# Attention scores dealt into ten visits a batch instead of twelve, over seven PSUM banks

## The chip, the cores and the metric

The kernel runs on one core of one Trainium2 chip. The metric is the time of one execution in microseconds (us) of device time; of several runs the median is given. Beside it stands a profile of one execution, which names every instruction with its engine, its line and its times. TensorE is called PE there, its weight loads PEld, VectorE DVE, ScalarE ACT, GpSimd POOL and SyncE SP.

## The reference

Every batch `b` of 32 holds 256 channels of 32 x 32 = 1024 tokens. They are normalized in groups of 8 channels, projected to queries, keys and values, and go through causal attention with 8 heads of 32 channels, in which a token sees only those before it; the result is added to the input.

```python
xf = _gn(x).reshape(B, C, S)                       # B 32, C 256, S 1024, all float32
q = einsum('oc,bcs->bos', q_w, xf) + q_b           # 8 heads x 32 channels
k, v = split(einsum('oc,bcs->bos', kv_w, xf) + kv_b)
mask = tril(ones((S, S)), -1)
scores = where(mask == 0, -10000, q k^T / sqrt(32))
attn = where(mask == 0, 0, softmax(scores))
out = x + attn v
```

## The kernel before

**Tiles of the array.** All matmuls are float32. A score product (`score`, L325) takes 32 rows (the channels of one head) and 64 columns (half of a block of 128 keys): the array is split into 8 tiles of 32 x 64, one for each of four heads and each half of a key block, and they work side by side. Projections (`project_qk` L264, `project_v` L280) and products with the values (`values`, L441) use tiles of 128 x 32, four side by side. Scores are laid out transposed: keys on partitions, queries along the row, so that one product of a tile is a run of query columns for 64 keys. Each product stands in the profile as two weight loads and two matmul records.

**Visits.** A batch has two groups `g` of four heads. The lower triangle of key blocks and query columns is dealt to six visits a group (`VISITS`, L612), twelve a batch (`N`). A visit has a long run of 512 query columns for each head and a short one of 256 columns (two of the six), or of 192 where a pair of diagonal blocks shares the room (`pair`, L309). For each tile this comes to 704 columns in visits 0, 1, 3 and 4 and to 768 in visits 2 and 5.

**PSUM.** `ps_s` has three buffers of two banks each. A visit takes all three: long runs of heads 0 and 1, long runs of heads 2 and 3, and the short runs of all four. Heads share a bank in the short runs, and tiles of different heads must not write one bank at the same time, so `scores` (L375) issues the short products of heads 2 and 3 first, lets them raise the semaphore `bank_free`, and has PE wait once for it before the short products of heads 0 and 1. The two banks left are `ps_o`, which gathers the products with the values (`acc`), and `ps_m` (`misc`), in which the projections are made; a few early ones use `ps_o` (`spare`, L161).

**The order of the work** is written out by hand (`manual_schedule`): each engine runs its instructions in the order in which the program issues them. In step `i` of the main loop (L785) come: the scores of visit `i`, with three exponentials on ACT (two of the long runs, L426, then the short one, L422) and the masking of diagonal blocks on POOL (L366); what is due `at` step `i`, above all one projection, which ACT copies out of PSUM (L276, L293); the products of visit `i - 1` with the values (`PRODUCTS`, L624); the additions of its exponentials to a running sum on DVE (`ADDS`, L639; L469); and what is due `after` it. `PROJECT` (L681) gives the steps of the twelve projections of a batch, five of them before the batch's own first step. Other lists place the loads, the normalization, the folding of the sums by DMA from POOL and SP and the last division on DVE. In the last batch the sums are made on PE instead (`sums`, L508).

Of the kernel before, what the change touches and what calls it, by code (L numbers as in the profile page):

```python
# [26 lines left out]
HALFBANK = HALF // 2  # L27
ROW = 64
# [4 lines left out]
def tile_norm_attention_residual(  # L33
# [69 lines left out]
    def unshifted():  # L103
        live = {}
        bank_free = tc.alloc_semaphore("bank_free")
# [15 lines left out]
        qkpool = tc.alloc_tile_pool(name="qkpool", bufs=3)  # L121
# [6 lines left out]
        pools = [xpool, work, qkpool, epool, small, dram, ps_s, ps_o, ps_m]  # L128

        def misc(name):  # L130
            return ps_m.tile([P, HALF], F32, tag="misc", name=name)


        def load_weights(junk):
# [5 lines left out]
            for n, w in enumerate((q_w, kv_w[0:C], kv_w[C : 2 * C])):  # L140
                live["wn", n] = epool.tile([P, 4, HALFBANK], F32, tag="eh", bufs=3, name=f"wn_{n}")[:, :NG, :C]
                nc.sync.dma_start(out=live["wn", n], in_=w.rearrange("(o p) c -> p o c", p=P))
# [17 lines left out]

        def spare(name):  # L161

            live["turn"] = live.get("turn", -1) + 1
            if live["turn"] in (1, 3, 5):
                return ps_o.tile([P, HALF], F32, tag="acc", name=name)
            return misc(name)
# [52 lines left out]
        def norm_mean(b):  # L219
            mv = live["mv", b]  # L220
            pm = misc(f"pm_{b}")
# [12 lines left out]
        def norm_variance(b):  # L234
            pv = misc(f"pv_{b}")
# [28 lines left out]
        def project_qk(b, g, n, hf):  # L264
# [5 lines left out]
            pp = spare(f"pp_{b}_{g}_{n}_{hf}")  # L270
# [9 lines left out]
        def project_v(b, n):  # L280
# [4 lines left out]
            pp = spare(f"ppv_{b}_{n}").rearrange("p (s c) -> p s c", c=C)  # L285
# [9 lines left out]
        def projections(b):  # L295

            qk = [[lambda g=g, hf=hf, n=n: project_qk(b, g, n, hf) for n in range(2)] for g in range(NG) for hf in range(NH)]
            v = [lambda n=n: project_v(b, n) for n in range(NB // 2)]
            return qk[0] + v[:1] + qk[1][:1] + v[1:2] + qk[1][1:] + qk[2] + v[:1:-1] + qk[3]

        def full(kb, first, width, at):

            return at, width, [[(c, kb, first, width, slice(at, at + width))] for c in (0, KEYS)]

        def pair(j, at):  # L309


            even, odd = 2 * j, 2 * j + 1
            c0, c1, c2, c3 = (at + n * KEYS for n in range(4))
            return at, 3 * KEYS, [
                [
                    (0, even, even * P, P, slice(c1, c3)),
                    (0, odd, odd * P, KEYS, slice(c0, c1)),
                ],
                [
                    (KEYS, odd, odd * P, P, slice(c0, c2)),  # L320
                    (KEYS, even, even * P + KEYS, KEYS, slice(c2, c3)),
                ],
            ]

        def score(b, g, bank, j, op):  # L325

            c, kb, first, width, cols = op
            rows = slice(HD * j, HD * (j + 1))
            return nc.tensor.matmul(  # L329
                bank[c : c + KEYS, cols], lhsT=live["k", b, g][rows, kb * P + c : kb * P + c + KEYS],  # L330
# [3 lines left out]
        def scores_of(b, g, bank_of, heads, entries, between=lambda: None, order=slice(None)):  # L334

            done = {}
            for _, _, halves in entries:
                for k, n in enumerate(list(range(max(map(len, halves))))[order]):
                    if k:
                        between()  # L340
                    for j in heads:
                        for c, ops in enumerate(halves):
                            if n < len(ops):
                                done.setdefault((j, c), []).append(score(b, g, bank_of(j), j, ops[n]))
            return done

        def part_of(b, g, bank, entry, of):

            at, _, halves = entry
            for j in (0, 1):  # L350
                for ((c, kb, first, _, cols),) in halves:
                    score(b, g, bank[:, j, :], j, (
                        c, kb, first + of.start, of.stop - of.start, slice(cols.start + of.start, cols.start + of.stop)
                    ))

        def mask(b, g, raw, j):


            hf, place = j // 2, (2 * j % 4) * P
            if ("e", b, g, "D", hf) not in live:  # L360
                live["e", b, g, "D", hf] = epool.tile(
                    [P, 4, HALF], F32, tag=("e0", "e")[hf], bufs=4, name=f"diagonal_{b}_{g}_{hf}"
                )
            square = live["e", b, g, "D", hf]
            for s in range(2):
                nc.gpsimd.affine_select(  # L366
                    out=square[:, :, place + s * P : place + (s + 1) * P],
# [612 lines left out]
```

## Time and profile before

| | |
|---|---|
| time, median of 3 runs (1792.47 to 1795.82) | 1792.5 us |
| span of the profiled execution, first to last instruction | 1791.2 us |
| PE busy | 1782.1 us |
| DVE busy | 1669.4 us |
| ACT busy | 1441.4 us |
| POOL busy | 897.9 us |

The span of the profiled execution is 1.3 us below the median. Busy time counts an engine as busy from the start of an instruction to its recorded end, and a matmul's end is modelled, so that a PE that is always busy need not be at its peak: what PE does is read from the starts of its phases in the timeline. The timeline merges neighbouring instructions of one line; its columns are the start, the length, the engine, the line and the operation, the tiles, and the count. Where one row joins several shapes, it carries the name of one of them.

### The profile page before, as it was taken

How to read it: one execution, taken by the hardware profiler on the slowest of the kernel's cores; microseconds unless marked ns; L12 is line 12 of the kernel's file. 1: busy time of each engine (PE TensorE's matmuls, PEld its weight loads, DVE VectorE, ACT ScalarE, POOL GpSimd, SP SyncE). 2: the span in 40 equal slices, each digit the busy share in tenths (PEclk: the TensorE clock that was granted, in tenths of full speed). 3: DMA queues.
4: the chain of work that ended last, by engine and by line, in shares of the span. 5: the costliest groups of instructions: out<-in, count | busy, mean ns of one | idle time of the engine just before them, and what ended most of it. 6: DMA issues, size and time to landing. Idle time of an engine off the chain costs nothing.

```text
span 1791.2 us, 81784 instructions
## 1 busy us (share of the span) xinstructions
PE 1782.1 (99%) x37036; PEld 936.1 (52%) x37036; DVE 1669.4 (93%) x1796; ACT 1441.4 (80%) x1928; POOL 897.9 (50%) x935
## 2 busy tenths in 40 slices
PE   9999999999999999999999999999999999999998
PEld 5555555555555555555555555555555555555554
DVE  4689999999999999999999999999999999999998
ACT  6888878888778788788887888877888878888785
POOL 2355554554555555545555555454455554554542
PEclk9999999999999999999999999999999999999999
DMA  2567766767677676676776676767766766777663
GB/s 72 105 117 142 137 133 135 148 138 147 128 142 138 137 141 138 132 144 142 142 138 134 137 142 138 150 129 140 139 145 131 141 136 135 149 138 141 133 109 98
DMA packets 92771, 240.21 MB, mean 134 GB/s; under 512 B 26272, under 2 KB 27792, under 8 KB 76544
## 3 DMA queue, kind: packets, MB, share of 16 engines
q0 software_dynamic: 17360, 100.58, 40.1%
q1 hardware_dynamic: 74912, 134.28, 25.9%
q8 instruction: 290, 4.75, 1.1%
q14 instruction: 65, 0.53, 0.1%
q10 hardware_dynamic: 144, 0.07, 0.0%
HBM read 69.90 MB, written 34.95 MB: 59 GB/s over the span
## 4 chain that ended last, share of the span: by engine, by line
PE 99%; DVE 0%; ACT 0%; issue 0%; POOL 0%; POOLq 0%
PE sT L329 31%; PE acc L451 28%; PE pp L173 27%; PE ppv L173 13%; PE pd L503 1%; PE busy L159 0%; PE wt L152 0%; ACT e L426 0%; DVE rb_last L576 0%; DVE rb_last L563 0%; DVE turned L560 0%; DVE acc L573 0%; DVE inv_last L562 0%; POOL ident masks.py:199 0%; PE pv L173 0%
## 5 line engine op out<-in xcount | busy, mean ns | idle before, releaser
L426 ACT ACTIVATE e<-sT 128x1024 f32<-128x1024 f32 x768 | 744.3, 1022 | 301.5 <-PE sT L329 298.8
L366 POOL TENSOR_SCALAR_AFFINE_SELECT diagonal<-eh 128x512 f32<-128x512 f32 x512 | 563.3, 1122 | 625.4 <-ACT eh L422 624.7
L469 DVE TENSOR_TENSOR e<-e,e 128x1024 f32<-128x1024 f32 x314 | 578.0, 1841 | 23.0 <-ACT v L293 3.5
L329 PE MATMUL sT<-q,k 32*64 32x64 f32 (+1 forms) x18928 | 577.9, 367 | 0.1
L329 PEld LDWEIGHTS sT<-q,k 32*64 32x64 f32 x18928 | 397.0, 131 | 203.8 <-PE sT L329 67.4
L173 PE MATMUL pp<-xn,wT 128*32 128x512 f32 x4096 | 492.3, 598 | 0.0
L451 PE MATMUL acc<-e,v 128*32 128x512 f32 (+3 forms) x4608 | 401.0, 450 | 0.0
L422 ACT ACTIVATE eh<-sT 128x768 f32<-128x768 f32 (+1 forms) x384 | 341.6, 890 | 0.0
L451 PEld LDWEIGHTS acc<-e,v 128*32 128x32 f32 x4608 | 149.2, 110 | 261.5 <-issue 239.0
L173 PE MATMUL ppv<-wT,xn 128*32 128x256 f32 x4096 | 247.5, 382 | 0.0
L469 DVE TENSOR_TENSOR diagonal<-diagonal,e 128x1536 f32<-128x1536 f32 x126 | 194.5, 1544 | 16.1 <-PE acc L451 6.5
L173 PEld LDWEIGHTS pp<-xn,wT 128*32 128x32 f32 x4096 | 107.0, 109 | 195.8 <-issue 163.7
L469 DVE TENSOR_TENSOR e<-e,eh 128x1024 f32<-128x1024 f32 x126 | 177.6, 1410 | 6.5
L451 PEld LDWEIGHTS acc<-diagonal,v 128*32 128x32 f32 x4096 | 120.9, 110 | 88.1 <-issue 68.2
L173 PEld LDWEIGHTS ppv<-wT,xn 128*32 128x32 f32 x4096 | 120.2, 109 | 80.0 <-issue 7.0
L469 DVE TENSOR_TENSOR e<-e,diagonal 128x2048 f32<-128x2048 f32 x63 | 144.0, 2285 | 18.9 <-POOL diagonal L366 18.7
L451 PE MATMUL acc<-diagonal,v 128*32 128x128 f32 x4096 | 158.9, 273 | 0.0
L205 POOL DMA_INDIRECT eight<-each,group_of x31 | 42.9, 1383 | 193.4 <-DMA each<-st 193.4
L262 ACT ACTIVATE xn<-x,shift,rstd 128x256 f32<-128x256 f32 x248 | 137.2, 614 | 0.8 <-POOL shift L247 0.8
L576 DVE SCALAR_TENSOR_TENSOR rb<-num,v_bias_col,x 128x256 f32<-128x256 f32 x248 | 121.5, 530 | 4.4
L482 POOL DMA_DIRECT2D e<-e x124 | 103.6, 835 | 42.6 <-issue 42.6
L482 POOL DMA_DIRECT2D diagonal<-diagonal x124 | 105.1, 847 | 0.7
(87 smaller groups left out, 1092.2 us busy)
## 6 DMA issues: line engine op xcount, KB each, us to landing
x<-in_x_dram SPq DMA_DIRECT2D x124, 256.0 KB, 3.8
diagonal<-diagonal POOLq DMA_DIRECT2D x62, 512.0 KB, 6.1
e<-e POOLq DMA_DIRECT2D x62, 512.0 KB, 5.7
rb<-inverses SPq DMA_DIRECT2D x124, 256.0 KB, 4.0
out_dram<-rb SPq DMA_DIRECT2D x124, 256.0 KB, 4.2
diagonal<-diagonal POOLq DMA_DIRECT2D x62, 256.0 KB, 4.6
folded<-diagonal SPq DMA_DIRECT2D x62, 256.0 KB, 5.1
e<-e POOLq DMA_DIRECT2D x62, 256.0 KB, 4.6
```

The costliest lines, as they stand in the source:

```text
L173: nc.tensor.matmul(out[part], lhsT=lhsT[:, part], rhs=rhs, start=start, stop=stop, skip_group_check=True)
L205: nc.gpsimd.indirect_dma_start(eight, None, live["each", b].rearrange("(m c) s -> m (c s)", c=CPG), bass.IndirectOffsetOnAxis(ap=group_of[ ...
L262: nc.scalar.activation(to, of, AF.Identity, bias=live["shift", b][:, g : g + 1], scale=rstd)
L329: return nc.tensor.matmul(bank[c : c + KEYS, cols], lhsT=live["k", b, g][rows, kb * P + c : kb * P + c + KEYS], rhs=live["q", b, g][rows, ...
L366: nc.gpsimd.affine_select(out=square[:, :, place + s * P : place + (s + 1) * P], in_=raw[:, :, (1 - s) * KEYS : (3 - s) * KEYS], pattern=[ ...
L422: exp = nc.scalar.activation(eh.rearrange("p (n bank) q -> p bank n q", n=2)[:, :, :, :narrow], short[:, :, :, :narrow], AF.Exp)
L426: nc.scalar.activation(e[:, 2 * a : 2 * a + 2, :wide], pairs[a][:, :, :wide], AF.Exp)
L451: nc.tensor.matmul(acc[HD * j : HD * (j + 1), of], lhsT=live["v", b][:, kb, h * HD : (h + 1) * HD], rhs=e[:, j, :], start=first, stop=last ...
L469: nc.vector.tensor_add(to, to, tile_of(b, g, at))
L482: nc.gpsimd.dma_start(out=total[:rows], in_=total[rows : 2 * rows], accum_op=ALU.add)
L503: nc.tensor.matmul(pd[HD * j : HD * (j + 1), of], lhsT=pick, rhs=e[:, j, :], start=start, stop=stop, skip_group_check=True,)
L576: nc.vector.scalar_tensor_tensor(blocks(rb, s), blocks(num, s, (start + s) % 2 == 1), v_bias_col[:, g : g + 1], blocks(xt[:, g, cols], s), ...
```

## The change

Each group of heads is visited five times instead of six, with 896, 832, 896, 896 and 896 columns for each tile. The score banks are four in `ps_s` (two buffers of two banks, long runs) and three in the new `ps_t` (`tri`): the short runs of the four heads, up to 384 columns each, lie one behind the other over three banks, so that heads 1 and 2 have pieces in two banks. The order of a visit's products is written as a string: `2e1` is the piece `e` of head 2 in bank 1 of `tri`, `3La` and `3Lb` are the first and the second half of head 3's long run, and `W` is a wait of PE for semaphore `bank_free[0]`, then `bank_free[1]`. The first pair of heads named (`sooner`) takes the first buffer of `ps_s`.

The bank `misc` is gone. A projection is made in a new buffer of `ps_s` (`room`), which is the one that held the visit's first two long runs, or in the bank of `acc` (`lone`). The products of the visit before with the values are split: one part ahead of the projection and one behind it. Visit 0 has no products of its own; visit 1 has those of both. At steps 1 and 6 of a batch there are two projections, `lone` and then `room`.

Key block rows 0 and 1 are masked where they stand; three pairs of blocks (2 and 3, 4 and 5, 6 and 7) share their room. DVE makes twelve additions a group instead of eleven, over the same number of columns, and in the last batch all but the last two visits' sums are made by additions, with fewer summing products on PE. Some pools have one buffer less (`qkpool`, `num`, `e`), the steps of all that is placed by hand are dealt anew for `N` = 10, and two waits before the values (`EVEN`) and the splitting of long runs in two visits (`SPLIT`) are gone.

```diff
-        bank_free = tc.alloc_semaphore("bank_free")
+        bank_free = [tc.alloc_semaphore(f"bank_free_{k}") for k in range(2)]
...
-        ps_s = tc.alloc_tile_pool(name="ps_s", bufs=3, space=PSUM)
+        ps_s = tc.alloc_tile_pool(name="ps_s", bufs=2, space=PSUM)
+        ps_t = tc.alloc_tile_pool(name="ps_t", bufs=1, space=PSUM)
         ps_o = tc.alloc_tile_pool(name="ps_o", bufs=1, space=PSUM)
-        ps_m = tc.alloc_tile_pool(name="ps_m", bufs=1, space=PSUM)
...
+        def lone(name):
+            return ps_o.tile([P, HALF], F32, tag="acc", name=name)
+
+        def room(name):
+            at = live.pop("room", None)
+            if at is None:
+                at = ps_s.tile([P, 2, HALF], F32, tag="sT", name=name)
+                live["room"] = at
+                return at[:, 0, :]
+            return at[:, 1, :]
...
+            early = [lone] if b == 0 else []
+            return [
+                qk(0, 0, 0, *early), qk(1, 0, 0), v(0, *early), v(1), qk(0, 0, 1), qk(1, 0, 1, lone),
+                qk(0, 1, 0), qk(1, 1, 0), v(2), v(3), qk(0, 1, 1), qk(1, 1, 1, lone),
             ]
...
+        def row(kb, blocks, more=()):
+            return [
+                ("o", 0, 0, kb + 1, (kb + 1) * P, KEYS), ("o", KEYS, 0, kb + 1, (kb + 1) * P, P),
+                ("e", 0, KEYS, kb, kb * P, blocks * P),
+                ("e", KEYS, P, kb, kb * P + KEYS, blocks * P - KEYS),
+            ] + list(more)
...
+            banks = [ps_s.tile([P, 2, HALF], F32, tag="sT", name=f"sT_{name}_{a}") for a in range(2)]
+            tri = ps_t.tile([P, 3 * HALF], F32, tag="tri", name=f"tri_{name}")
...
+                if isinstance(op, int):
+                    live["free", op] = live.get(("free", op), 0) + list(ends.values()).count(op)
+                    wait = nc.tensor.wait_ge(bank_free[op], live["free", op])
...
+            for a in range(2):
+                step = heads[a][1] - heads[a][0]
+                nc.scalar.activation(e[:, heads[a][0] : heads[a][1] + 1 : step, :], banks[a], AF.Exp)
+            exp = nc.scalar.activation(
+                eh[:, :, :wide], tri.rearrange("p (j q) -> p j q", q=SHORT)[:, :, :wide], AF.Exp
             )
...
+        WHOLE = "1s0 2s1 3s2 0L 2L 1L 3L W 0s0 1s1 W 2s2"
         VISITS = [
...
+            (0, 0, both("s", 1, P, 3 * P), (0, 2), WHOLE),
+            (0, HALF, row(2, 2), (2, 3), "2e2 1e1 3La 0e0 0o0 3Lb 2L 1L 0L W 3e2 3o2 2e1 W 1o0 2o1 1e0"),
+            (
+                1, HALF, row(4, 1, both("x", 5, 6 * P, P + KEYS, P + KEYS)), (2, 3),
+                "1e1 2x2 0x0 3Lb 0o0 1x1 2Lb 0e0 3La 1Lb 2La W 0Lb 3o2 1La 3x2 W 2o1 0La 2e1 1o0 3e2 1e0 2x1",
+            ),
+            (
+                2, HALF, row(6, 2, both("x", 5, 7 * P + KEYS, KEYS, 2 * P + KEYS)), (0, 1),
+                "3x2 1o0 2o1 0Lb 1e0 2e1 3e2 1Lb 3o2 0La 2Lb 1La 3Lb W 0o0 2La 0e0 3La 1e1 0x0 W 2e2 2x2 1x1",
+            ),
+            (3, HALF, both("s", 4, 5 * P, 3 * P), (0, 2), WHOLE),
         ]
...
-        PROJECT = (-5, -4, -3, -2, -1, 0, 1, 2, 3, 4, 5, 6)
-        PREPARE = (-12, -11, -10, -10, -9, -8, -7, -6, -5, -3)
-        SUMS = (3, 7, 10, 13)
+        PROJECT = (-4, -3, -2, -1, 0, 1, 1, 2, 3, 4, 5, 6)
+        PREPARE = (-11, -10, -9, -9, -8, -7, -6, -5, -2, -1)
+        SUMS = (4, 6, 8, 11)
+        STACK = (6, 9, 11, 14)
...
                 if i < B * N:
                     scores(*divmod(i, N))
+                b, v = divmod(i - 1, N)
...
+                if i:
+                    values(b, v, 0)
                 for f in at.pop(i, ()):
                     f()
...
                 if i:
-                    for _ in range(EVEN.count((i - 1) % N) if i < B * N - N else 0):
-                        nc.tensor.wait_ge(bank_free, live["free"])
-                    values(b, v)
-                    if b < B - 1 or v not in SUMMED or v == 1:
+                    values(b, v, 1)
+                    if b < B - 1 or v < N - 2:
                         add_keys(b, v)
```

The products with the values of the visits: visit 1 has 512 and 384 columns ahead of the projection and three of 128 behind it, visits 2 and 3 have 512 and 512 (visit 3 behind it in four pieces), visit 4 has 512 and 384, and three of 128.

More of the change, by code (lines that the diff above doesn't have):

```diff
@@ L27 @@
 HALFBANK = HALF // 2
+SHORT = 3 * P
 ROW = 64
@@ L540, in with_scores @@
         def with_scores(ahead=0):
-            nc.sync.wait_ge(bank_free, live["free"] + 4 * ahead)
+            v = live["visit"]
+            more = [n for i in range(v + 1, v + 1 + ahead) for n in PROGRAMS[i % len(VISITS)][1].values()]
+            nc.sync.wait_ge(bank_free[0], live["free", 0] + more.count(0))
         def spread_inverses(b, h):
```

376 lines of the change are left out of this document (181 added, 195 removed).

## The prediction

> **What bounds the kernel now.** I read the page's first section, then the timeline of PE over a few visits in the middle, then the engine windows of one batch.
>
> ```profile
> span 1791.2 us, 81784 instructions
> PE 1782.1 (99%) x37036; PEld 936.1 (52%) x37036; DVE 1669.4 (93%) x1796; ACT 1441.4 (80%) x1928; POOL 897.9 (50%) x935
> ```
>
> ```profile
> 899.23 1.49 PE L329 MATMUL sT<-q,k 32*64 32x64 f32 x64
> 900.65 1.92 PE L173 MATMUL pp<-xn,wT 128*32 128x512 f32 x16
> 902.39 1.05 PE L451 MATMUL acc<-e,v 128*32 128x384 f32 x16
> ...
> 903.80 1.47 PE L329 MATMUL sT<-q,k 32*64 32x128 f32 x48
> 905.21 1.92 PE L173 MATMUL pp<-xn,wT 128*32 128x512 f32 x16
> 906.95 1.05 PE L451 MATMUL acc<-e,v 128*32 128x384 f32 x16
> ...
> 908.36 1.55 PE L329 MATMUL sT<-q,k 32*64 32x256 f32 x32
> 909.84 1.92 PE L173 MATMUL pp<-xn,wT 128*32 128x512 f32 x16
> 911.58 0.61 PE L451 MATMUL acc<-e,v 128*32 128x256 f32 x8
> ...
> 912.56 1.46 PE L329 MATMUL sT<-q,k 32*64 32x64 f32 x56
> 913.95 1.93 PE L173 MATMUL ppv<-wT,xn 128*32 128x256 f32 x32
> 915.70 1.47 PE L451 MATMUL acc<-e,v 128*32 128x512 f32 x16
> ...
> 917.53 1.46 PE L329 MATMUL sT<-q,k 32*64 32x64 f32 x56
> ...
> 954.21 1.49 PE L329 MATMUL sT<-q,k 32*64 32x64 f32 x64
> ```
>
> ```profile
> 899.20:954.20 55.00, 55.00 (x1156) 28.86 (x1152) 52.71 (x57) 44.94 (x60) 28.78 (x29) 1.00 0.70 139
> ```
>
> The first and the last timeline row are visit 0 of two batches: one batch takes 54.98 us. Starts subtracted, a projection takes 1.74 us for 1024 columns, or 1.70 ns a column. At that rate the score phases (1.42, 1.41, 1.48, 1.39 us for 704, 704, 768 and 704 columns a tile) contain 0.17 to 0.22 us each that is no streaming, and the products with the values (1.41, 1.41, 0.98, 1.83 us for 768, 768, 512, 1024 columns) contain 0.10 each, the change back to score tiles. No row has a wait in brackets: PE streams columns, and a visit costs about 0.3 us beside them. The window (span, PE, PEld, DVE, ACT, POOL busy, clock) shows DVE next, 52.71 of 55, then ACT, 44.94; the clock is 1.00.
>
> **The sum without waits, a batch.** Projections stay: 12 x 1.74 = 20.9. Values stay at 4608 columns a group: 7.83 us, but with four changes of tiles instead of six, 0.40; where visit 1's two projections run straight into scores another 0.10: 2 x 8.33 = 16.7. Scores grow from 4352 to 4416 columns a tile and group (rows 0 and 1 no longer share a diagonal): 7.51 us. For what is no streaming I take 0.18 in the two visits with two or three pieces a tile, as in the 768 rows; 0.21 in visit 1, with three or four, as in the 704 rows; and 0.25 in visits 2 and 3, with five or six, by the same step a piece. No row has so many pieces; the bounds are 0.17 and 0.30. That is 1.07 a group, so 2 x 8.58 = 17.2. Together 54.7 us; the same formula gives 54.9 for before, where 54.98 was measured. **So two visits fewer are worth only 0.26 us a batch, 8.3 us in all.** The last batch has 4160 summing columns instead of 5760: 2.7 us less at 1.70 ns.
>
> **What hid the copies, and what is late next.** Before, a projection had a bank to itself, and scores three buffers. Now `room` takes the buffer of the first pair, X; the next visit takes Y first and X as its second pair. So the second pair waits for a copy that ACT can begin only when the projection is done.
>
> ```profile
> 15.79 0.61 PE L173 MATMUL ppv<-wT,xn 128*32 128x256 f32 x8
> 16.34 0.47 PE L329 MATMUL sT<-q,k 32*64 32x64 f32 x20
> 16.47 0.58 ACT L293 COPY v<-ppv 128x512 f32<-128x512 f32 x1 [1.04 <-PE ppv L173]
> ```
> ```profile
> L276 ACT ACTIVATE q<-pp,qk_bias 128x512 f32<-128x512 f32 x128 | 89.9, 702 | 0.9 <-PE pp L173 0.9
> ```
> ```profile
> 1754.60 0.61 PE L451 MATMUL acc<-eh,v 128*32 128x256 f32 x8
> 1755.15 2.12 PE L329 MATMUL sT<-q,k 32*64 32x128 f32 x48
> 1757.19 1.92 PE L173 MATMUL pp<-xn,wT 128*32 128x512 f32 x16
> ```
> ```profile
> 1756.17 0.58 PEld L329 LDWEIGHTS sT<-q,k 32*64 32x64 f32 x24 [0.50 <-ACT eh L422]
> ```
> ```profile
> 1755.31 0.82 ACT L422 ACTIVATE eh<-sT 128x768 f32<-128x768 f32 x1
> ```
>
> The first three rows are a projection that runs straight into scores on an idle ACT: the copy begins 0.13 us after the scores. The last three fences show the price of such a wait, in the last batch: the copy ends at 1756.13, a weight load follows at 1756.17, so 0.04 later, and this score phase takes 2.04 us where its like takes 1.41. Everything behind the waiting load on PE is held too.
>
> (a) *Visit 1 into visit 2.* Step 1 has no values between its second projection and the scores of visit 2. The bank is free 0.13 + 0.70 + 0.04 = 0.87 us into the phase. The string needs it at `1Lb`, when head 1's tiles have done 256 columns: 0.04 + 0.44 = 0.48. All tiles carry 896 columns, so nothing absorbs it: 0.39 us. Behind `1Lb` in PE's queue stand `2La`, the first `W` and `0Lb`; head 0 runs dry at 384 columns, 0.69.
>
> (b) *Visit 0 into visit 1.* The queries of the second half are projected at step 0 and are needed by `3La`, third in the string. Between lie 384 columns, 0.65, and the change of tiles, 0.10; the copy ends 0.10 + 0.13 + 0.70 + 0.04 = 0.97 after the projection, 0.22 into the phase. Head 3 would start at 0.04: 0.18 us. `0e0` and `0o0` wait behind it.
>
> (c) *Visit 4's projection* needs the first exponential done.
>
> ```profile
> 909.54 1.94 ACT L426 ACTIVATE e<-sT 128x1024 f32<-128x1024 f32 x2 [1.32 <-PE sT L329]
> 911.36 1.03 ACT L422 ACTIVATE eh<-sT 128x1024 f32<-128x1024 f32 x1
> ```
>
> The phase at 908.36 gives its first pair after 512 columns (0.87), and ACT starts 1.18 in: 0.31 later. In `WHOLE`, head 2 does 256 + 512 columns first, so ACT starts at 1.31 + 0.31 = 1.62 and ends 1.02 later; with 0.04 PE may go at 2.68. It is there at 896 x 1.70 + 0.18 + 512 x 1.70 = 2.57: 0.11 us.
>
> The other steps hold by the same arithmetic. Visit 4's copy frees its bank about when visit 0 asks for it; `tri` is free 1.82 (909.54 to 911.36) plus 1.46 (estimate: 1.03 plus 512 columns at 0.82 ns) after the first exponential, at 4.9 us of 5.3. PE's two `W` wait for short products done by 0.65, while every tile has long work queued: nothing, or 0.2 us where a queue runs dry. Dropping `EVEN` frees nothing, for its scores are issued long before.
>
> Each of the three can be nothing, if the copy comes earlier than I think, or the whole 0.87, 0.22 and 0.3, if the tiles cannot fill around it. I take the values worked out. (a) occurs 63 times, (b) 64, (c) 63: 24.6 + 11.5 + 6.9 = 43.0 us.
>
> **Costed at nothing, with the cover.** ACT: ten long exponentials and five short ones a group instead of twelve and six, with 17664 columns instead of 17408; the rows' spacing (0.91 for 1024) makes that equal. DVE has one addition more a group:
>
> ```profile
> L469 DVE TENSOR_TENSOR e<-e,e 128x2048 f32<-128x2048 f32 x126 | 299.9, 2380 | 10.4 <-ACT e L426 0.5
> L469 DVE TENSOR_TENSOR e<-e,eh 128x1024 f32<-128x1024 f32 x126 | 177.6, 1410 | 6.5
> ```
>
> These give 0.95 ns a column and 0.44 fixed: 0.9 us a batch, 53.6 in all. It fits into 56.1, but a batch below 54 would meet it. On POOL the eight selections of a group stay; its folds move to steps 4, 6, 8 and 11, and each holds the selections behind it until DVE has added. The latest, at step 6, follows 5.7 us of additions begun in step 5 and ends at the start of step 7, some 4 us before the next mask. SP's stacks, loads and `with_scores` keep their order, and the first semaphore rises once a visit.
>
> The Trainium skill says under PSUM Bottleneck (TensorEngine Tiling, Performance Considerations) that tiling speeds TensorE but not the emptying of PSUM, whose copy may become the bottleneck. By that rule the change, which takes a buffer away, is wrong in kind; as a throughput bound the window above does not bear it out (ACT 44.94 of 55), as a delay it is (a).
>
> **The sum.** -8.3 - 2.7 + 43.0 = +32.0. Start and end I leave even: the first scores come one projection sooner and meet an exponential in step 1 (0.8), and the last three visits wait for exponentials about as the last five did. 1791.2 + 32.0 = 1823.2 for the span; the runs' median lies 1.3 above it: **1824.5 us**, its own range 1806 to 1842.
>
> **Rivals.**
> *Faster: the copies keep ahead.* If the `room` bank and the queries are there when PE asks, only -11.0 is left: 1781.5. It decides at 0.17 us of wait a group, (11.0 / 64), where I count 0.68. For it: in the middle rows no phase waits for ACT. Against it: there nothing used a copied bank within a visit. 0.22.
> *Only (a) bites*; the strings cover (b) and (c): -11.0 + 24.6, 1806. 0.15; a further 0.06 for waits that just cancel the gain, within 0.2% (3.6 us, about what a measurement here can tell from no change).
> *Products start strictly in order.* Then in `WHOLE` `1L` cannot begin before `2L`, at 256 columns instead of 128: 0.22 us on four phases a batch, 28 us: 1852.
>
> ```profile
> 880.85 0.45 PE L329 MATMUL sT<-q,k 32*64 32x256 f32 x4
> 880.88 1.09 PE L329 MATMUL sT<-q,k 32*64 32x512 f32 x16
> ```
>
> Against it, from two windows of one phase: the 512-wide products began at 880.88, when only four of the eight records of the 256-wide ones, issued before them, had begun. 0.07. The Trainium skill states that order in TensorE: Matmul & The Clock Gate, What overlaps and what doesn't: matmuls start and end in program order; these two rows speak against it across tiles.
> *DVE becomes the bound.* 53.6 busy and as much waiting as now (54.98 - 52.71 = 2.3) is 55.9, just under 56.1; were the waits to double, 58.2: 3.2 x 32 - 2.7 = +100, 1893. 0.05.
> *The forecast*: 0.45.
>
> **Range.** Faster by over 0.2%: 0.22, the first rival. Within 0.2%: 0.06. Slower: 0.45 + 0.15 + 0.07 + 0.05 = 0.72. To leave out two in ten the range takes in the rival at 1781.5, with the lower bound of the phase overheads, and ends at 1848.
>
> **What would show it.** Right: score rows of visit 2 about 2.1 us long with a weight load inside them that waited for ACT's copy of a projection; visit 1's about 1.8; batches 56.1 us apart; 0.1 us ahead of the fourth visit's projection. Wrong: score phases of 1.70, 1.62 and 1.77 us with no waiting load, batches near 54.7, or waits of ACT for DVE.

## The result and the profile after

| | before | after |
|---|---|---|
| time, median of 4 runs each, same chip | 1793.55 us (1792.47 to 1795.82) | 2061.96 us (2055.97 to 2069.57) |
| ratio, with its 95% interval | | 1.1499 (1.1471 to 1.1527) |
| span of the profiled execution | 1791.2 us | 2059.8 us |
| mean granted clock of TensorE | 1.00 | 0.958 |

The change makes the kernel 15% slower. The prediction had the sign, and missed the size by 237 us. These lines are from the page of the profile after: the span, the busy times, two groups of PE and ACT. In a group's line, the first number behind the bar is its busy time, the next the mean length in ns, and behind the second bar stands the idle time ahead of it and what ended that.

```profile
span 2059.8 us, 81280 instructions
...
PE 1878.6 (91%) x36892; PEld 1003.2 (49%) x36892; DVE 1675.1 (81%) x1864; ACT 1468.6 (71%) x1736; POOL 872.8 (42%) x935
...
L176 PE MATMUL pp<-xn,wT 128*32 128x512 f32 x4080 | 538.7, 662 | 155.2 <-ACT num L475 155.2
...
L475 ACT COPY num<-acc 128x512 f32<-128x512 f32 x127 | 74.4, 586 | 186.6 <-DVE rb L598 186.6
```

Busy times have hardly moved on DVE (1669.4 before) and ACT (1441.4), but PE is now idle for a tenth of the span. Two idle times, which no line of before has, form a chain: the copy `num` on ACT waits 186.6 us for DVE, and projections on PE wait 155.2 us for that copy. The view of waits (engine and line, what it waited for, total, times, longest) says how often:

```profile
ACT num L475 <- DVE rb L598: 186.6, 30, 8.3
...
PE pp L176 <- ACT num L475: 155.2, 30, 7.2
```

Thirty times is once a batch, from the third batch to the last. The windows of the engines show it from one batch to the next (span, busy time of PE, PEld, DVE, ACT and POOL, granted clock, share of the DMA engines):

```profile
1000.00:1027.89 27.89, 27.89 (x578) 15.29 (x574) 26.57 (x26) 23.78 (x30) 11.49 (x14) 1.00 0.77 151
1027.89:1033.60 5.71, 5.71 (x101) 2.90 (x97) 5.57 (x7) 4.73 (x6) 1.95 (x4) 1.00 0.69 132
1033.60:1046.30 12.70, 8.14 (x99) 3.02 (x95) 7.09 (x11) 4.41 (x6) 4.90 (x5) 0.73 0.46 105
1046.30:1063.70 17.40, 17.40 (x412) 10.41 (x414) 13.70 (x17) 13.43 (x16) 9.08 (x9) 1.00 0.46 88
```

The first row is half a batch, the second group's five visits, with PE always busy: twice 27.89 is 55.78 us, a batch without the stall. In the third row, step 1 of the next batch, PE does 8.14 us of work in 12.70, at a clock of 0.73; in every other stretch the clock is 1.00. Now the timelines of ACT, of DVE and of PE around that step (start, length; in brackets the idle time ahead and its releaser):

```profile
1033.08 0.69 ACT L279 ACTIVATE q<-pp,qk_bias 128x512 f32<-128x512 f32 x1 [0.34 <-PE pp L176]
1039.37 0.59 ACT L475 COPY num<-acc 128x512 f32<-128x512 f32 x1 [5.61 <-DVE rb L598]
1039.86 1.95 ACT L439 ACTIVATE e<-sT 128x1024 f32<-128x1024 f32 x2
```

```profile
1030.63 2.27 DVE L484 TENSOR_TENSOR e<-e,e 128x2048 f32<-128x2048 f32 x1
1033.01 2.00 DVE L484 TENSOR_TENSOR e<-e,eh 128x1536 f32<-128x1536 f32 x1
1035.11 1.47 DVE L484 TENSOR_TENSOR e<-e,diagonal 128x1024 f32<-128x1024 f32 x1
1036.50 1.27 DVE L192 BATCH_NORM_STATS2 st<-x 128x6 f32<-128x512 f32 x2
1037.70 0.67 DVE L590 TENSOR_TENSOR num<-num,rb 128x512 f32<-128x512 f32 x1
1038.40 0.88 DVE L593 SCALAR_TENSOR_TENSOR rb<-num,v_bias_col,x 128x256 f32<-128x256 f32 x2
1039.20 0.14 DVE L598 COPY rb<-x 128x1 f32<-128x1 f32 x1
...
1049.59 1.76 DVE L484 TENSOR_TENSOR e<-e,eh 128x1536 f32<-128x1536 f32 x1 [8.72 <-issue]
```

```profile
1033.05 0.62 PE L466 MATMUL acc<-diagonal,v 128*32 128x128 f32 x16
1040.01 6.33 PE L176 MATMUL pp<-xn,wT 128*32 128x512 f32 x32 [4.56 <-ACT num L475]
```

`num` is the buffer into which ACT copies the finished products with the values, four a batch, and which `finish` on DVE reads a batch later. The diff takes one of its eight buffers away. With seven, the eighth copy, the last of batch b+1, goes into the buffer of the first of batch b. That copy is issued in step 0 of batch b+2 and the `finish` that reads the buffer in step 1, behind step 0's additions. So ACT, with the exponentials of step 1 behind the copy in its queue, stands still until DVE has done 5.87 us of additions (1030.63 to 1036.50), two statistics and the division (1037.70 to 1039.34); the copy begins at 1039.37. PE cannot project either, for the bank that the copy is to empty is the one that the projection wants. When it gets it, the two projections take 6.33 us: the clock is at half.

```profile
1040.00:1046.40 6.40, 6.39 (x42) 1.51 (x50) 0.86 (x2) 3.62 (x4) 3.10 (x4) 0.57 0.38 105
```

The whole difference of the spans can be told from starts on PE: of the first scores of the second batch and of the last batch, first before, then after.

```profile
73.47 1.49 PE L329 MATMUL sT<-q,k 32*64 32x64 f32 x64
...
1723.93 1.49 PE L329 MATMUL sT<-q,k 32*64 32x64 f32 x64
```

```profile
76.00 0.56 PE L377 MATMUL tri<-q,k 32*64 32x128 f32 x6
...
1978.91 0.57 PE L377 MATMUL tri<-q,k 32*64 32x128 f32 x6
```

| where | before | after | difference |
|---|---|---|---|
| start and first batch | 73.47 | 76.00 | +2.5 |
| thirty batches between | 1650.46 | 1902.91 | +252.5 |
| last batch, to the end of the span | 67.3 | 80.9 | +13.6 |

Of the 252.5 us, 30 x (55.78 - 55.02) = 22.8 is the regular batch; 55.02 is the mean of the kernel before, in which one batch of the thirty takes 56.05 us and the others 54.98. Twenty-nine of the thirty stalls lie in these batches, the last one in the last batch. The 29 steps, each taken against the 5.36 us of the same step in the second group, sum to 214.5, of which 150.3 is PE's wait. The rest, 64.2, is work at half the clock: behind the 29 restarts the clock stays at half for 126.8 us in all, and half of that is 63.4. Some 15 us are left: short pauses at other places, to which the experiments come back.

### The profile page after: what moved, and what is told of

Its sections match the earlier page's. It is cut to its first block, busy times and chain, and to the rows that moved or that the text cites. A ratio compares the mean times of both kernels' runs of the same rounds, so it can differ in the third digit from the quotient of the medians.

```text
span 2059.8 us, 81280 instructions
## 1 busy us (share of the span) xinstructions
PE 1878.6 (91%) x36892; PEld 1003.2 (49%) x36892; DVE 1675.1 (81%) x1864; ACT 1468.6 (71%) x1736; POOL 872.8 (42%) x935
## 3 DMA queue, kind: packets, MB, share of 16 engines
q8 instruction: 289, 4.73, 1.0%
## 4 chain that ended last, share of the span: by engine, by line
PE 73%; DVE 17%; issue 4%; DMA 4%; ACT 1%; POOL 1%; DVEq 0%; SPq 0%; POOLq 0%
PE pp L176 22%; PE acc L466 21%; PE tri L377 12%; DVE e L484 11%; PE sT L377 10%; PE ppv L176 9%; DMA rb<-inverses 3%; DVE rb L593 2%; DVE st L192 1%; DVE num L590 1%; ACT num L475 1%; DVE turned L510 1%; DVE rows L511 1%; DMA each<-st 0%; DMA e<-e 0%
## 5 line engine op out<-in xcount | busy, mean ns | idle before, releaser
L384 POOL TENSOR_SCALAR_AFFINE_SELECT diagonal<-eh 128x512 f32<-128x512 f32 x384 | 405.2, 1076 | 723.6 <-ACT eh L440 722.4
L484 DVE TENSOR_TENSOR e<-e,eh 128x1536 f32<-128x1536 f32 x381 | 450.3, 1182 | 299.5 <-issue 255.9
L176 PE MATMUL pp<-xn,wT 128*32 128x512 f32 x4080 | 538.7, 662 | 155.2 <-ACT num L475 155.2
L377 PE MATMUL tri<-q,k 32*64 32x128 f32 (+4 forms) x12416 | 574.8, 299 | 9.1 <-issue 5.7
L377 PE MATMUL sT<-q,k 32*64 32x256 f32 (+1 forms) x7424 | 565.9, 464 | 0.4 <-ACT q L279 0.3
L377 PEld LDWEIGHTS tri<-q,k 32*64 32x64 f32 x12416 | 413.4, 131 | 184.8 <-ACT v L296 65.1
L484 DVE TENSOR_TENSOR e<-e,e 128x2048 f32<-128x2048 f32 x190 | 449.5, 2366 | 14.9 <-PE acc L466 7.8
L440 ACT ACTIVATE eh<-tri 128x1536 f32<-128x1536 f32 (+1 forms) x320 | 453.5, 1417 | 1.3 <-PE tri L377 1.2
L466 PE MATMUL acc<-e,v 128*32 128x512 f32 x2560 | 341.4, 602 | 0.0
L484 DVE TENSOR_TENSOR e<-e,diagonal 128x1024 f32<-128x1024 f32 x190 | 249.8, 1315 | 20.2 <-DVE e L484 0.5
L475 ACT COPY num<-acc 128x512 f32<-128x512 f32 x127 | 74.4, 586 | 186.6 <-DVE rb L598 186.6
L176 PEld LDWEIGHTS ppv<-wT,xn 128*32 128x32 f32 x4096 | 126.8, 109 | 158.1 <-ACT e L439 83.2
L466 PE MATMUL acc<-eh,v 128*32 128x384 f32 (+3 forms) x3072 | 197.7, 344 | 0.0
```

Source lines behind the costliest of these rows:

```text
L176: nc.tensor.matmul(out[part], lhsT=lhsT[:, part], rhs=rhs, start=start, stop=stop, skip_group_check=True)
L377: return nc.tensor.matmul(to[c : c + KEYS, at : at + width], lhsT=live["k", b, g][rows, kb * P + c : kb * P + c + KEYS], rhs=live["q", b, ...
L384: nc.gpsimd.affine_select(out=to, in_=of, pattern=[[0, 4], [(1, -1)[odd], P]], compare_op=ALU.is_gt, fill=0.0, base=0, channel_multiplier= ...
L440: exp = nc.scalar.activation(eh[:, :, :wide], tri.rearrange("p (j q) -> p j q", q=SHORT)[:, :, :wide], AF.Exp)
L466: nc.tensor.matmul(acc[HD * j : HD * (j + 1), of], lhsT=live["v", b][:, kb, h * HD : (h + 1) * HD], rhs=e[:, j, :], start=first, stop=last ...
L475: nc.scalar.copy(num, acc)
```

## The experiments

Times are medians; each ratio is against the kernel before, run on the same chip. "Batch" is the mean distance of the thirty batches between the second's first scores and the last's, "pauses" is 30 times that less the kernel's own undisturbed batch (55.78 us unless another is given). These two columns come from one profiled execution each, and executions differ: the times of `num8` lie 7.3 us apart, those of `light` 0.9. In `early`, `tail` and `spaced` the last column also holds waits of PE for ACT, of about 17, 3 and 69 us.

| run | time, us | ratio (95% interval) | batch | pauses |
|---|---|---|---|---|
| `num8` | 1845.69 | 1.0294 (1.0277 to 1.0311) | 56.54 | 22.8 |
| `early` | 1855.32 | 1.0343 (1.0320 to 1.0365) | 56.87 | 32.7 |
| `late` | 1900.76 | 1.0600 (1.0582 to 1.0617) | 58.22 | 30 (batch 57.22) |
| `moved` | 1830.49 | 1.0210 (1.0193 to 1.0227) | 55.98 | 20 (batch 55.31) |
| `dealt` | 1818.03 | 1.0138 (1.0123 to 1.0154) | 55.49 | 14 (batch 55.03) |
| `apart` | 1853.33 | 1.0339 (1.0322 to 1.0355) | 56.55 | 23.2 |
| `shift` | 1860.79 | 1.0376 (1.0362 to 1.0390) | 56.52 | 22.1 |
| `tail` | 1853.29 | 1.0324 (1.0305 to 1.0343) | 56.76 | 29.3 |
| `light` | 1825.84 | 1.0189 (1.0175 to 1.0203) | 55.78 | 0.1 |
| `spaced` | 1898.62 | 1.0578 (1.0561 to 1.0594) | 58.33 | 99 (batch 55.03) |

### Is it the buffer of `num`?

`num8` gives the buffer back, and takes one from the masked squares (`d`) to make room:

```diff
-                square = epool.tile([P, 4, 2 * P], F32, tag="d", bufs=3, ...)
+                square = epool.tile([P, 4, 2 * P], F32, tag="d", bufs=2, ...)
-                    num = work.tile([P, HALF], F32, tag="num", bufs=7, ...)
+                    num = work.tile([P, HALF], F32, tag="num", bufs=8, ...)
```

> Edit: eight buffers for num instead of seven, paid for with two for the diagonal squares instead of three. Theory (seven buffers make ACT's copy of the last values of a batch wait for a division that DVE does one step later, and everything behind it on ACT and PE waits too): the wait of ACT on that copy is gone, no half clock, the batches are 55.8 us apart as the undisturbed half batches of the changed kernel (27.89) say, and the time is about 1826 us (before + 30 x 0.8 + 2.9 at the start + 7 at the end). Rival (DVE is simply too late in this schedule, and the buffer only names where it is felt): the wait moves to the next buffer and the time stays above 1950 us.

`early` keeps seven buffers, and has DVE finish the first quarter of batch b ahead of the additions of step 0:

```diff
-        SPREAD = (1, 1, 3, 4)
-        FINISH = (N + 11, N + 11, N + 12, N + 13)
+        SPREAD = (1, 1, 2, 2)
+        FINISH = (N + 10, N + 11, N + 12, N + 13)
...
-                        when(v, lambda b=b, n=n, later=later: finish(b, n, later=later), after)
+                        when(v, lambda b=b, n=n, later=later: finish(b, n, later=later), after if late or n else at)
```

> Edit: seven buffers for num are kept; the first division of a batch goes one step earlier, ahead of that step's additions on DVE, with the inverses it needs loaded by then. Theory (it is the order of copy and division that makes the wait, not the number of buffers as such): again batches of about 55.8 us and 1826 us in all, give or take 8. Rival (seven buffers are too few in any order): as the changed kernel, near 2060 us.

Both take the wait away and 207 to 216 us with it; the clock is back at 0.996 in `num8`, and its two projections of a step 1 take 3.64 us, not 6.33:

```profile
756.87 3.64 PE L176 MATMUL pp<-xn,wT 128*32 128x512 f32 x32
```

In `early` the view of waits still has a trace of the copy waiting for DVE:

```profile
ACT num L475 <- DVE rb L598: 1.6, 3, 0.7
```

So it is not the seven buffers as such, and not the two in place of three of `d`, but that the copy stands one step ahead of the division it waits for. Both kernels come out above the 1826 us that the theory gave, by 20 to 30 us.

### Is the copy out of the lent bank priced rightly?

`late`, on top of `num8`, makes the copies out of the lent bank in the steps before visit 2's scores twice, so that the bank comes free one copy later:

```diff
+            twice = bank is room and live.get("visit", 0) % len(VISITS) == 1
+            for _ in range(2 if twice else 1):
-            nc.scalar.activation(
+                nc.scalar.activation(
```

> Edit: num8, and ACT copies the room projection of steps 1 and 6 out of PSUM twice, so that its bank is free about 0.59 us later. Theory (the score phase of visit 2 waits for that bank): its 2.12 us become 2.7, a batch grows by 1.2 us, the time by about 37 us to 1863. Rival (the phase is long because of its many pieces and two waits): 2.12 us stay and the time is that of num8.

Visit 2's first score products and its first product with the values, in the timeline of PE after the change, then in that of `late` (line numbers there are two higher):

```profile
1011.06 0.41 PE L377 MATMUL tri<-q,k 32*64 32x64 f32 x6
...
1013.18 0.64 PE L466 MATMUL acc<-e,v 128*32 128x512 f32 x4
```

```profile
840.78 0.41 PE L379 MATMUL tri<-q,k 32*64 32x64 f32 x6
...
843.62 0.64 PE L468 MATMUL acc<-e,v 128*32 128x512 f32 x4
```

The phase is 2.12 us long, and 2.84 with one more copy: the copy's own length, 0.7, is paid in full. That is how a copy that ends the phase behaves, and (a) of the prediction stands. The undisturbed batch is 57.22 us, 2 x 0.72 more: 43 us over thirty batches, where 37 had been expected. Most of the rest of the 55 us is pauses.

`moved`, on top of `num8`, shifts products with the values to the other side of a projection: visit 3's 64 columns of (H, 3) ahead of that of step 4, visit 4's 384 columns of (H, 4) behind that of step 0, and 128 columns in return:

```diff
-                1, [(("L", 3, Q(0, 4)), 2, Q(0, 4))], [
-                    (("H", 2, Q(1.5, 3)), 5, Q(2, 3.5)), (("H", 3, Q(2.5, 3)), 5, Q(3.5, 4)),
+                1, [(("L", 3, Q(0, 4)), 2, Q(0, 4)), (("H", 3, Q(2.5, 3)), 5, Q(3.5, 4))], [
+                    (("H", 2, Q(1.5, 3)), 5, Q(2, 3.5)),
...
-                1, [(("L", 4, Q(0, 4)), 3, Q(0, 4)), (("H", 4, Q(0, 3)), 4, Q(1, 4))], [
-                    (("H", 3, Q(1.5, 2.5)), 6, Q(3, 4)), ...
+                1, [(("L", 4, Q(0, 4)), 3, Q(0, 4)), (("H", 3, Q(1.5, 2.5)), 6, Q(3, 4))], [
+                    (("H", 4, Q(0, 3)), 4, Q(1, 4)), ...
```

> Edit: num8, and of the products with the values one of 64 columns goes ahead of the projection at steps 4 and 9, and at steps 0 and 5 one of 128 goes ahead and one of 384 behind it. Theory (visit 1's scores wait for the query copy, step 4's projection for the first exponential): visit 1's score phase shrinks from 1.79 to about 1.6 us and step 4 by 0.1, together 0.29 a half batch, 18 us: about 1808. Rival (these phases are long in themselves): the time of num8.

Time falls by 15 us, to 1830 where 1808 had been expected; the undisturbed batch falls by 0.47 us, where 0.58 had been expected. The step whose projection waited for the first exponential goes from 5.38 to 5.28 us, the 0.1 of (c), and visit 1's score phase from 1.78 to 1.59, the 0.18 of (b). `dealt` adds another order for visit 2's products, which asks for the lent bank later:

```diff
-                1, HALF, row(4, 1, ...), (2, 3),
-                "1e1 2x2 0x0 3Lb 0o0 1x1 2Lb 0e0 3La 1Lb 2La W 0Lb 3o2 1La 3x2 W 2o1 0La 2e1 1o0 3e2 1e0 2x1",
+                1, HALF, row(4, 1, ...), (1, 2),
+                "1e1 0x0 3o2 2Lb 1x1 0o0 3e2 2La 0e0 3x2 1L 0L 3L W 2o1 2e1 2x1 W 2x2 1o0 1e0",
```

> As moved, and the score products of visit 2 are put in another order: the pair of heads whose long bank was lent to projections comes later, so that the copy out of that bank (0.87 us into the scores) has more products ahead of the one that needs it. By the prediction's own model of wait (a) the wait falls from 0.39 to about 0.18 us a visit, the score phase from 2.12 to about 1.9 us, twice a batch: 13 us less than moved. Rival (visit 2's phase is long because of its many short products and not because of the lent bank): 2.1 to 2.2 us as in moved, time within 3 us of it.

The phase falls from 2.18 and 2.04 us (first and second group) to 1.96 and 1.90, the time by 12 us. With the three waits cut to what is left, the undisturbed batch is 55.03 us, and that of the kernel before is 54.98. Something is still to be had: visit 3, which has as many pieces as visit 2, takes 1.74 us. If visit 2 took no longer, the batch would be 0.38 us shorter, 54.65 (an estimate from these three phases), about the 54.7 of the prediction's sum without waits. No run shows that batch.

### Where are the other 20 us?

In `num8`, single steps are up to 4 us longer than their like; nearly all of the 22.8 us lies in the steps of visit 3, steps 3 and 8 of a batch. PE at two such places, with the engine windows of the second:

```profile
769.50 0.33 PE L377 MATMUL tri<-q,k 32*64 32x64 f32 x4 [1.11 <-issue]
```

```profile
1704.71 0.32 PE L377 MATMUL tri<-q,k 32*64 32x64 f32 x2 [1.96 <-issue]
1704.96 1.55 PE L466 MATMUL acc<-e,v 128*32 128x512 f32 x8
1706.26 3.18 PE L176 MATMUL ppv<-wT,xn 128*32 128x256 f32 x32
```

```profile
1706.30:1709.30 3.00, 3.00 (x40) 1.57 (x36) 2.69 (x1) 0.22 (x1) 2.70 (x2) 0.58 1.00 185
```

The releaser is "issue": PE waited for nothing that the profile shows. The second pause, 1.96 us, is followed by work at half the clock. PE's code, the instructions that it is to run, comes by DMA, in 289 packets of 16 KB for some 73,800 instructions, 255 each. What stands ahead of each pause is a 16 KB packet of the instruction queue (page of the profile: "q8 instruction: 289, 4.73"). In the trace's list of packets one ended 1.33 us ahead of the restart at 769.50 and 1.61 ahead of that at 1704.71. From 60 us on there are 13 pauses of over 0.15 us ahead of the last batch (at one the view names ACT as the releaser), and each ends 1.29 to 1.61 us behind such a packet, though the packets lie 6.3 us apart on average. A count of PE's instructions in the trace says more: when any of the 13 begins, 194 plus a whole multiple of 256 have started, so that all 13 stand at one place of a piece of code of 256 instructions. So PE had run out of code. The 13 pauses sum to 10.8 us, 9.8 of it in the thirty batches. Of the rest of the 22.8 us, 1.7 is the clock behind the second pause above; most of what is left lies in steps 3 and 8 as well, where the weight loads pause and PE works off what it has (in the sixteenth batch, step 3 is 1.08 us too long, with 0.95 us of PEld idle for "issue" and 0.04 of PE). Three runs asked why the code is late.

`shift` moves PE's code against its packets by half a packet:

```diff
+            for _ in range(128):
+                nc.tensor.drain()
             keep_busy(14)
```

> As num8, with 128 empty instructions more on TensorE before its first matmul, which moves its code against the 16 KB pieces in which it arrives. Theory (a piece of code that is due in a score phase comes late): a batch of about 2306 instructions is 9.0 pieces long, so a bad meeting of the two lasts for many batches; moved by half a piece, the pauses come in other batches and other steps, and their sum changes by 5 us or more in either direction. Rival (the pauses have to do with data or buffers): the same batches and the same steps 3 and 8 pause, time within 2 us of num8's.

The pauses move. In `num8` they lie at step 3 in four batches in a row (655 to 827 us) and at step 8 in six (1417 to 1705); in `shift` they lie at step 8 in five batches in a row (581 to 811) and there is one in all behind 1400. A cause in data or buffers would have left them in place; and 9 of 10 again end 1.29 to 1.61 us behind a packet, at the same count of 194 (the tenth is a wait for ACT). But the sum stays, 22.1 against 22.8 us, and a change of 5 us had been expected. Of the 7.1 us between the spans, 6.8 are the empty instructions themselves, ahead of the second batch; the medians differ by 15, on two chips on which the kernel before differs by 1.6, and what the rest is has not been found.

`apart` moves two of SP's transfers, an output and a spread of inverses, away from others that go at the same step:

```diff
-        SPREAD = (1, 1, 3, 4)
+        SPREAD = (1, 2, 3, 4)
...
-                        later = ... when(*((first + 2 * N + 3, send) if n < 2 else ...
+                        later = ... when(*((first + 2 * N + 2 + n, send) if n < 2 else ...
```

> As num8, and two transfers are moved: the output of a batch's first half, which left together with that of the second half before the step after next, leaves one step earlier, and the second of the four spreads of inverses one step later. In num8 nearly all of the time over a regular 55.78 us a batch lies in the steps that follow these pairs (steps 3 and 8: about 20 us over the run), and each of TensorE's pauses there ends 1.3 to 1.6 us after a packet of the instruction queue. Theory (the code of TensorE arrives late because it lies behind bunched transfers): most of the 20 us goes, 10 to 18 us less than num8's 1845.7, and the excess in steps 3 and 8 falls below 10 us. Rival (the pauses belong to the order of the products or to two diagonal buffers instead of three): time and the place of the pauses stay as in num8, within 3 us.

A miss: no gain, and still 23.2 us of pauses, a part of them now in step 2. `light` cuts most of the traffic of GpSimd's queue, and so leaves out a part of each sum:

```diff
-            nc.gpsimd.dma_start(out=total[:rows], in_=total[rows : 2 * rows], accum_op=ALU.add)
+            nc.gpsimd.dma_start(out=total[:2], in_=total[rows : rows + 2], accum_op=ALU.add)
```

> As num8, and each of the eight folds of a batch, in which GpSimd's queue adds one half of a tile's rows to the other, adds 2 rows instead of 64 or 32; the denominators are then sums over a part of the keys, all else is computed as before. GpSimd issues as many transfers as in num8 and waits for them as before, but 768 KB a batch-quarter, the 37.5% of the DMA engines' span that its queue took, is gone. Theory (code for TensorE arrives late because the DMA engines are busy with other transfers): the excess over the regular steps, 22.7 us in num8 between the second batch and the last, falls below 6 us, and the time to about 1825 us. Rival (the pauses belong to the rate at which the score products use up code, whatever else is moved): the excess stays at 18 us or more and the time within 5 us of num8.

First and last row of PE for `num8`, then for `light`, as above, and behind each the line of the page for the queue of the folds, q0 (packets, MB, share of 16 engines); for `light` that of the other transfers, q1, stands with it:

```profile
75.57 0.56 PE L377 MATMUL tri<-q,k 32*64 32x128 f32 x6
...
1771.77 0.56 PE L377 MATMUL tri<-q,k 32*64 32x128 f32 x6
```

```profile
q0 software_dynamic: 17360, 100.58, 37.5%
```

```profile
74.01 0.56 PE L377 MATMUL tri<-q,k 32*64 32x128 f32 x6
...
1747.49 0.56 PE L377 MATMUL tri<-q,k 32*64 32x128 f32 x6
```

```profile
q1 hardware_dynamic: 74912, 134.28, 26.0%
q0 software_dynamic: 9424, 7.16, 2.6%
```

1673.48 / 30 is 55.78 us: with the folds gone from the DMA engines, thirty batches are undisturbed to a tenth of a microsecond, and the time falls to the 1826 us that was expected. The 20 us are code that reaches PE late, and it is late with the folds and not without them. The packets themselves are no slower with the folds (1.02 us in the median, 1.05 in `light`); they start later: by the same count of instructions, the latest of `num8` starts 130 instructions of PE later than the latest of `light`. What holds the start back, a DMA engine that is taken or something else, the traces do not show.

`spaced`, on top of `dealt`, keeps all transfers and issues each second fold a step later (and the copy behind it one or two):

```diff
-                        when(v + 1, lambda b=b, n=n: fold(b, n, HD), after)
-                        when(first + STACK[n], lambda b=b, n=n: stack(b, n), at if n else after)
+                        when(v + 1 + (b < B - 2), lambda b=b, n=n: fold(b, n, HD), after)
+                        when(first + STACK[n] + (b < B - 2) * (2, 1, 1, 1)[n], lambda ..., at if n else after)
```

> As dealt, and the second fold of each tile (64 rows to 32) is issued two steps after the first instead of one, as in the kernel before, so that no fold is issued right ahead of the two score phases that pause (visit 3, steps 3 and 8); the copies to one place follow one or two steps later. In dealt the steps of a middle batch lie 13 us over their own medians, 12 of them in steps 3 and 8. Theory (it is the folds in flight at those steps that make the code late, and their times can be chosen): the excess falls below 5 us and the time from 1818 to about 1808 us. Rival (the sum of what is moved decides, or other steps pause in their place): excess 10 us or more, time within 4 us of dealt, or above it where a buffer is held longer than the exponentials can wait.

Slower by 80 us, and inconclusive: exponentials now wait for the tile that the late copy still reads, and PE behind them.

```profile
ACT e L439 <- DMA folded<-e: 84.9, 36, 4.2
...
PE pp L176 <- ACT e L439: 45.7, 40, 2.5
```

Step 8 pauses less than in `dealt` (3.1 for 8.0 us) and step 3 more (9.6 for 4.3). Whether the folds can be timed so that code comes through is open, and so is why the kernel before, which moves the same bytes, has not one such pause.

### The end

The last batch is 9.2 us longer in `num8` than before (76.5 and 67.3). `tail` gives sums back to PE that DVE had got, to spare DVE 7.6 us of additions:

```diff
-                    when(first + 9, lambda: sums(2, WHOLE_OF[2:3], False))
+                    when(first + 7, lambda: sums(2, FIRST_HALF, False), after)
...
-                    if b < B - 1 or v < N - 2:
+                    if b < B - 1 or v < N - 4:
```

(`FIRST_HALF` lists the tiles of visits 5 and 6; `REMAINING`, for the last bank, gets those of visit 7.)

> As num8, and in the last batch VectorE no longer adds the keys of the second half's first queries (steps 5 to 7 of the batch): TensorE sums their tiles for the denominators, some 1.5 us of products more for one bank and 1.4 us for the other. VectorE is spared about 7.6 us of additions ahead of its last divisions, and TensorE waited 7.4 us for them. Theory (the end is set by VectorE's additions in the last batch): 4 to 6 us less than num8, and the last wait of TensorE falls from 7.4 to under 3 us. Rival (it is the four divisions of the batch before that hold VectorE up, or the sums on TensorE cost as much): within 1.5 us of num8.

PE's last wait for DVE (by way of POOL), before, in `num8` and in `tail`:

```profile
PE pc L599 <- POOL rows_last L595: 0.3, 1, 0.3
```

```profile
PE pc L616 <- POOL rows_last L612: 7.4, 1, 7.4
```

```profile
PE pc L616 <- POOL rows_last L612: 4.6, 1, 4.6
```

The wait shrinks by 2.8 us, to 4.6 and not to under 3, and PE's sums grow by about as much (1472 columns, 2.5 us at 1.70 ns): the last batch takes 75.6 us in place of 76.5, 0.9 less, where 4 to 6 had been expected. For the end the rival was right; what is moved from DVE comes back on PE. The time is 7.6 us above that of `num8`. Between the two spans it is 5.5: 0.9 less at the end and 6.5 more in the thirty batches, by pauses and waits for ACT that this edit was not meant to touch.

No kernel of these beats the kernel before. The best, `dealt`, is at 1.0138: in its span, 0.4 us more at the start and first batch, 14.2 in the middle, nearly all of it pauses (13.7), and 9.2 at the end.

## Why the prediction was wrong

**Two visits fewer, -8.3 us, and the three waits, +43.** These terms were about right together. Forecast were batches 56.1 us apart, measured 55.78 where nothing else disturbs; a score phase of about 2.1 us in visit 2 (2.12), of about 1.8 in visit 1 (1.78), and 0.1 us at visit 4's projection (0.10 by `moved`). Over thirty batches the regular part is +22.8 us, where the two terms give +33 (30 x (1.36 - 0.26)); each score phase came out 0.01 to 0.04 us shorter than forecast. (a), (b) and (c) are each shown by a run: `late` with `dealt`, and `moved`. Of the rivals, "the copies keep ahead" and "only (a) bites" fall with them; a strict order of products falls too, for the `WHOLE` phases take 1.69 us, where 896 columns at 1.70 ns are 1.52 and leave no room for 0.22 beside the 0.18 of overhead; DVE is not the bound, for `dealt` runs the same additions in batches of 55.03.

**The step that failed is "Costed at nothing, with the cover".** It went through ACT, DVE, POOL and SP by their busy time and by the place of folds, and left out the buffers of SBUF. The diff's `num`, 8 to 7, has no word in it. It should have asked for each pool that shrinks: which reader must have finished before the writer may start, and does that reader stand ahead of the writer in the steps? Here the copy of step 0 waited for a division of step 1. The prediction did name "waits of ACT for DVE" among the signs that it was wrong, and that is the line of 186.6 us. `num8` and `early` show the cause: 207 to 216 of the 237 us missed. Another part of the price, some 64 of the 214.5 us, is the clock, of which the prediction said only that it is 1.00; a PE idle for 4.56 us did the next 6.4 at 0.57.

**"Start and end I leave even", and -2.7 for fewer sums on PE.** With the buffer restored the end is 9.2 us longer, not 2.7 shorter, and the first batch 2.1. The additions that replace those sums are on DVE, which reaches the last division 7.4 us late; `tail` shows that moving them back does not pay either. The prediction counted the columns that PE loses and gave no cost to the additions that DVE gains, for which the last batch has no idle time: in `num8` DVE is busy for 46.8 of the 48.5 us from 1790 to 1838.5.

**No term for the pauses.** Some 15 us after the change, 23 in `num8`, from code that comes late (after the change, too, all seven pauses of "issue" stand at the count of 194). The prediction had no view for it: in the profile before PE never waits for "issue". The Trainium skill says in Runtime: NRT & Kernel Launch, Instruction fetch mechanics, that the sequencer fetches the next 16 KiB block while it runs the current one, and that crossing a block is mostly hidden. The 16 KB packets are in the trace, and before it is so; with `num8` it costs 22.8 us, and 0.1 when the folds are cut.

## What to carry over

Where a change takes a buffer from a ring, find for the copy that first reuses it the last reader of the old content, and compare their places in the order of issue: if the reader comes later, an in-order engine stops, whatever its share of busy time. Price a stall of the engine that sets the time with what follows it, the clock too. And before splitting work among fewer, denser phases, take the regular batch from the middle of a profile and ask whether there is a gain at all: here ten visits with their waits cut as far as `dealt` cut them give 55.03 us, twelve gave 54.98.

## What the hardware showed unasked

In the profile after, the clock goes to 0.5 once at each of the thirty stalls, for 6.83 us in 18 of them and for 3.41 us in 12, never another length, with idle times of PE of 4.6 to 7.2 us; in most it does so before PE starts again. The Trainium skill states in TensorE: Matmul & The Clock Gate, What's actually happening, that the clock follows a free-running window of about 3.4 us; one and two of these are what the trace has. One pause of 1.96 us in `num8` also brought 3.41 us at 0.5; its other twelve, of 0.18 to 1.87 us, did not. Length alone does not decide it: one of 1.96 us in the kernel after brought none, and one of 1.79 in `early` brought 3.41.

With other transfers in flight PE's code came late here, and that on DMA engines that are by no means full. The step with the pause at 769.50, and the one before it, in the windows of `num8` (the last two columns are the DMA engines' share and GB/s):

```profile
760.40:766.60 6.20, 6.20 (x150) 3.56 (x146) 5.82 (x9) 4.51 (x5) 4.10 (x5) 1.00 0.66 118
766.60:773.30 6.70, 5.59 (x138) 3.30 (x134) 6.46 (x11) 4.66 (x6) 3.75 (x3) 1.00 0.72 144
```

With the engines in use for 0.66 and 0.72 of the time, PE stood for 1.11 us; with the folds cut, it had no such pause in any of the thirty batches. But the share is not the whole of it: the kernel before, at 0.70 in the prediction's row, has none either.
